# Attention over channels in float32r halves stacked four times along the contraction

## The chip, the cores and the metric

The kernel runs on one core of one Trainium2 chip. The metric is the device time of one execution in microseconds; the time of the kernel before is the median of three runs. Beside it there is one profiled execution with a trace of every instruction. The engines are named as in the profile: PE (TensorE, matrix products), PEld (its weight loads), DVE (VectorE), ACT (ScalarE), POOL (GpSimd) and SP (SyncE, which issues the transfers here).

## The reference

The program is a decoder of four layers with three sublayers each: an attention, a cross-attention and a feed-forward part. After each of them the rows are added to their input and normalized. `x` and the context `ctx` have the shape 64 x 64 x 256 (64 sequences of 64 rows). The change concerns the fifth sublayer, the cross-attention of the second layer, in which the 256 channels attend to each other and the 64 rows of a sequence are split into 8 heads of 8 rows:

```python
def _L1_xattn_ref(q, k, v, gamma):          # q = x, k = v = ctx_2048
    N_HEAD = 8
    B, Dq, Lq = q.shape                     # 64, 64, 256
    Dv, Lk = (v.shape[-2], v.shape[-1])
    h = N_HEAD
    dq = Dq // h                            # 8
    dv = Dv // h
    qh = q.reshape(B, h, dq, Lq)
    kh = k.reshape(B, h, dq, Lk)
    vh = v.reshape(B, h, dv, Lk)
    scale = 1.0 / jnp.sqrt(jnp.asarray(dq, dtype=q.dtype))
    qk = jnp.einsum('bhdq,bhdl->bhql', qh, kh) * scale
    sm = jax.nn.softmax(qk, axis=-1)
    ret = jnp.einsum('bhql,bhdl->bhdq', sm, vh)
    ret = ret.reshape(B, Dv, Lq)
    return gamma * ret
...
x = _layernorm(x + _L1_xattn_ref(x, ctx_2048, ctx_2048, L1_xattn_gamma), axis=-1)
```

There are 512 blocks (64 sequences x 8 heads). Each is a score matrix of 256 x 256 whose contraction is only 8 long.

## The kernel before

**Order of the whole.** The rows lie in eight groups of 512, each held in on-chip memory as `X[g]` (128 partitions, 4 tiles of 128 rows, 256 channels). The sublayers run one after the other: the first attention, then the first cross-attention and feed-forward together (`l0_both`), the second attention (`l1_attn`), then the attention over channels (`l1_xattn`) and its feed-forward (`l1_ffn`). Inside these functions the order of PE, ACT, DVE and (in `l0_both` and `l1_attn`) POOL is written out by hand: each engine works its instructions off in the order of the program, and one that waits holds up all behind it. The transfers on SP are placed by the scheduler, and SP too works them off in one queue.

**Tiles and blocks of the fifth sublayer.** A tile is 128 rows, or two sequences, or 16 blocks; there are 32. The 128 rows of PE's array are used as four strips of 32, one for each of four blocks at a time (index `r`), and the loop over `j` (0 to 3) goes through the rest. A step of the loop (L1652, `for step in range(n + 2)`) takes a new tile `step` and an old one `step - 2`; for each `j` there is one unit: two calls of `scored` (a half each, two strips for the new tile and the two others for the old one), then `weighted` for the unit before.

- `scored` (L1531) makes for the new tile the scores with the queries on the partitions (`sq`, L1547), two products of 128 x 256 a block, of which DVE takes the negated maximum of each row (`mc`, L1552). For the old tile it makes the transposed scores, keys on the partitions (`sk`, L1550), of which ACT takes the exponential (`e`, L1558).
- The maxima enter the transposed scores as a ninth row of the contraction: row 8 of each strip of the context's tile `cr` holds ones, row 8 of the rows' tile `xr` the negated maxima. `move` (L1561) brings them there: PE transposes `mc`, DVE copies it, SP stores it to memory and loads it back in its place. That happens one unit into the next step, so the old tile is two steps behind the new one.
- `weighted` (L1579) multiplies the exponentials with the values (`ret`, L1586; four blocks side by side, 32 columns of the array each), with a column of ones for the sums; ACT copies `ret` out at each `j` (L1590), and `store` writes the tile to memory.
- `load` (L1517) fetches a tile: 8 rows of context and of `x` a block, from `ctx` itself and from a copy of `X[g]` that is written to memory for it (`xd`, L1520). The four buffers of the tiles were cleared or set to one ahead (L1499, L1501).

All products here are float32. The trace records each of them as two, one for each half of the weights. All eight banks of the accumulators are one ring (`bank`, eight buffers): `sq`, `sk`, `ret` and the transposed maxima take the next free one.

**Around it.** In `l0_both` the feed-forward runs in units of 128 hidden columns, six a group (`HC`); `halved` (L1166) splits the turned rows into two float32r halves, `xhi` and `xlo`, in two buffers each. In `l1_attn` a loop of 12 iterations takes the eight groups through six stages. Each stage takes its memory from a pool, and the pool of `l1_both` waits, at its first write, for the last reader of what lay there before.

## Time and profile before

| | us |
|---|---|
| median of three runs | 4140.58 |
| lowest and highest run | 4131.2 and 4144.52 |
| the profiled execution | 4137.55 |
| its span from the first to the last instruction | 4135.8 |
| PE, PEld busy | 3900.5 (94%), 2594.9 (63%) |
| DVE, ACT, POOL busy | 2984.5 (72%), 2260.6 (55%), 1505.2 (36%) |

Busy time of the groups of the fifth sublayer, from the profile's costliest groups (a group's busy time counts overlapping instructions once):

| line | engine | what | count | busy us | mean ns |
|---|---|---|---|---|---|
| L1547 | PE | `sq` | 2048 records | 274.1 | 403 |
| L1550 | PE | `sk` | 2048 records | 253.4 | 394 |
| L1586 | PE | `ret` | 2048 records | 139.4 | 387 |
| L1552 | DVE | maxima | 512 | 317.5 | 683 |
| L1558 | ACT | exponentials | 512 | 265.6 | 609 |

PE's records overlap, as matrix products are pipelined and their ends are modelled: what one costs is seen in the distance between the starts of two, not in its duration. The same holds in part for DVE and ACT, where one instruction starts some 0.1 us before the modelled end of the last. A granted clock of 1.00 is the full one for PE, 0.50 is half. In the whole span it was 0.98 in the mean.

### The profile page before, as it was taken

How to read it: one execution, taken by the hardware profiler on the slowest of the kernel's cores; microseconds unless marked ns; L12 is line 12 of the kernel's file. 1: busy time of each engine (PE TensorE's matmuls, PEld its weight loads, DVE VectorE, ACT ScalarE, POOL GpSimd, SP SyncE). 2: the span in 40 equal slices, each digit the busy share in tenths (PEclk: the TensorE clock that was granted, in tenths of full speed). 3: DMA queues.
4: the chain of work that ended last, by engine and by line, in shares of the span. 5: the costliest groups of instructions: out<-in, count | busy, mean ns of one | idle time of the engine just before them, and what ended most of it. 6: DMA issues, size and time to landing. Idle time of an engine off the chain costs nothing.

```text
span 4135.8 us, 74789 instructions
## 1 busy us (share of the span) xinstructions
PE 3900.5 (94%) x28788; PEld 2594.9 (63%) x28808; DVE 2984.5 (72%) x5916; ACT 2260.6 (55%) x4654; POOL 1505.2 (36%) x1604
## 2 busy tenths in 40 slices
PE   8979988989998999989999999999999899999997
PEld 5646666666675555546666666666666666666765
DVE  6855658888684687877777777777776677777775
ACT  5645445667534577554444444444444476767765
POOL 4411121332441111115555555555543333433432
PEclk9989998999999999999999999999999999999999
DMA  2210012333200000031111111111121100000000
GB/s 73 85 35 16 16 55 56 75 79 72 78 1 13 1 1 1 11 133 29 29 27 26 27 31 27 27 26 27 31 72 54 47 22 22 24 24 22 23 20 11
DMA packets 112657, 149.68 MB, mean 36 GB/s; under 512 B 17636, under 2 KB 76196, under 8 KB 110888
## 3 DMA queue, kind: packets, MB, share of 16 engines
q1 hardware_dynamic: 111336, 143.27, 12.6%
q8 instruction: 230, 3.77, 0.4%
q10 hardware_dynamic: 960, 1.57, 0.2%
q14 instruction: 131, 1.07, 0.1%
HBM read 71.64 MB, written 30.95 MB: 25 GB/s over the span
## 4 chain that ended last, share of the span: by engine, by line
PE 43%; DVE 9%; ACT 2%; issue 1%; POOL 1%; DMA 0%; DVEq 0%; POOLq 0%; ACTq 0%
PE p L2116 19%; PE acc L2473 5%; PE acc L2739 4%; PE qT L561 2%; PE s L2411 2%; PE kT L561 1%; PE y L2441 1%; PE h L449 1%; PE yt L561 1%; PE s L2665 1%; DVE s L2672 1%; PE pt L561 1%; PE o L502 1%; PE y L2711 1%; DVE s L2671 1%
## 5 line engine op out<-in xcount | busy, mean ns | idle before, releaser
L1552 DVE TENSOR_REDUCE mc<-sq 128x2 f32<-128x512 f32 x512 | 317.5, 683 | 64.1 <-PE sk L1550 62.8
L555 POOL TENSOR_TENSOR rstd<-rstd,neg_half 128x1 f32<-128x1 f32 (+1 forms) x187 | 145.2, 777 | 600.1 <-DVE rstd L553 583.2
L1558 ACT ACTIVATE e<-sk 128x512 f32<-128x512 f32 x512 | 265.6, 609 | 113.1 <-PE sk L1550 91.8
L555 POOL TENSOR_TENSOR hrq<-hrq,neg_half 128x4 f32<-128x4 f32 (+1 forms) x192 | 234.4, 1221 | 246.4 <-DVE hrq L553 240.2
L1547 PE MATMUL sq<-l1x 32*128 32x256 f32 x2048 | 274.1, 403 | 4.9 <-DVE mc L1552 3.4
L555 POOL TENSOR_TENSOR hrk<-hrk,neg_half 128x4 f32<-128x4 f32 x160 | 187.8, 1174 | 228.4 <-DVE hrk L553 173.2
L1550 PE MATMUL sk<-l1x 32*128 32x256 f32 x2048 | 253.4, 394 | 0.5 <-DVE mc L1552 0.5
L2116 PE MATMUL p<-l3a_wq,xt 128*128 128x512 f32 x512 | 243.7, 599 | 9.7 <-DVE v L542 8.4
L2116 PE MATMUL p<-l3a_wk,xt 128*128 128x512 f32 x512 | 247.9, 607 | 0.0
L1547 PEld LDWEIGHTS sq<-l1x 32*128 32x128 f32 x2048 | 207.7, 193 | 57.7 <-DVE mc L1552 22.9
L2116 PE MATMUL p<-l3x_wq,xt 128*128 128x512 f32 x512 | 241.3, 594 | 0.8 <-DVE k L2577 0.8
L2739 PE MATMUL acc<-l3x_wo,yt 128*128 128x256 f32 x1024 | 235.7, 383 | 5.2 <-DVE yt L2723 3.5
L2116 PE MATMUL p<-l3a_wv,xt 128*128 128x512 f32 x512 | 233.2, 598 | 0.6 <-DVE k L542 0.4
L2473 PE MATMUL acc<-l3a_wproj,yt 128*128 128x256 f32 x1024 | 232.1, 380 | 0.6 <-DVE yt L542 0.3
L2473 PEld LDWEIGHTS acc<-l3a_wproj,yt 128*128 128x128 f32 x1024 | 194.1, 190 | 53.9 <-issue 29.2
L2739 PEld LDWEIGHTS acc<-l3x_wo,yt 128*128 128x128 f32 x1024 | 193.2, 191 | 44.2 <-issue 6.7
L1550 PEld LDWEIGHTS sk<-l1x 32*128 32x128 f32 x2048 | 189.4, 187 | 6.4 <-issue 2.9
L561 PEld LDWEIGHTS qT<-ident,q 128*128 128x128 f32 x1024 | 121.7, 141 | 98.4 <-issue 77.1
L2457 POOL TENSOR_TENSOR hry<-hry,neg_half 128x8 f32<-128x8 f32 x64 | 106.2, 1659 | 179.2 <-DVE hry L2453 174.7
L561 PE MATMUL qT<-ident,q 128*128 128x128 f32 x1024 | 156.7, 276 | 6.7 <-DVE hlo L413 5.4
L1586 PE MATMUL ret<-e,vt 128*32 128x256 f32 x2048 | 139.4, 387 | 18.9 <-DVE mc L1552 18.1
L2116 PEld LDWEIGHTS p<-l3a_wv,xt 128*128 128x128 f32 x512 | 92.1, 190 | 97.4 <-issue 82.0
(444 smaller groups left out, 10405.0 us busy)
## 6 DMA issues: line engine op xcount, KB each, us to landing
vs<-v SPq DMA_DIRECT2D x308, 128.0 KB
l3x_kv<-kv SPq DMA_DIRECT2D x28, 256.0 KB
x<-in_x SPq DMA_DIRECT2D x8, 512.0 KB
ct<-in_ctxT SPq DMA_DIRECT2D x8, 512.0 KB
cn<-in_ctx SPq DMA_DIRECT2D x8, 512.0 KB
l_x<-x SPq DMA_DIRECT2D x8, 512.0 KB
l1x<-in_ctx SPq DMA_DIRECT2D x128, 32.0 KB
l1x_x<-x SPq DMA_DIRECT2D x8, 512.0 KB
```

The source lines that it names most:

```text
L555: nc.gpsimd.tensor_tensor(out, out, self.neg_half[:, :n], ALU.pow)
L561: self.nc.tensor.transpose(ps[:, j * P : (j + 1) * P], blk, self.ident)
L1547: nc.tensor.matmul(ps[:, n, :], x_[rows, j, part], c_[rows, j, :], start=True, stop=True)
L1550: nc.tensor.matmul(ps[:, n, :], c_[rows, j, part], x_[rows, j, :], start=True, stop=True)
L1552: nc.vector.tensor_reduce(mc[new % 2][:, ra + k, 2 * j : 2 * j + 2], ps, AX.X, ALU.max, negate=True)
L1558: nc.scalar.activation(es[rb + k], ps, AF.Exp, scale=scale)
L1586: nc.tensor.matmul(ret[32 * r : 32 * r + 32, :], vt[i % 2][:, lc, 4 * r + j, :], es[r][:, lc, :], start=lc == 0, stop=lc == 1,)
L2116: self.nc.tensor.matmul(ps, lhs(c), w(c, cols), start=c == 0, stop=c == 1 and bias is None)
L2411: nc.tensor.matmul(ps[half(b), h * S : (h + 1) * S], qT[:, h % 4, half(b)], kT[:, h % 4, half(b)], start=True, stop=True,)
L2457: nc.gpsimd.tensor_tensor(r, r, self.neg_half[:, :8], ALU.pow)
L2473: nc.tensor.matmul(acc[:, :D], yts[h % 2][:, h // 2, :], wp[n // 8][:, (n % 8) * D : (n % 8 + 1) * D], start=n == 0, stop=n == 15,)
L2739: nc.tensor.matmul(acc[:, :D], yts[h % 2][:, h // 2, :], w.o[n // 8][:, (n % 8) * D : (n % 8 + 1) * D], start=n == 0, stop=n == 15,)
```

## The change

Rows and context of the fifth sublayer are no longer multiplied in float32. Each is split into two float32r halves, `hi` (the rounded value) and `lo` (what is left), and a block's contraction of 8 rows becomes 32: row `k` of four carries the half `k // 2` of `x` and the half `k % 2` of the context, so that one product of a strip sums all four combinations. The halves are made early and kept in memory: those of the context in the feed-forward stage of the first layer, those of `x` at the end of the second attention, by `halves_kept` (a cast on ACT, a subtraction on POOL, eight stores). `load` then needs eight transfers of 128 KB a tile. Nothing is cleared ahead any more, and a constant (`in8`) goes.

The maxima are no longer a row of the contraction. They are split into halves too (`mhi` by ACT, `mlo` by DVE, a store and a load each) and a product of its own lays them under both parts of `sk`: two rows of ones against the two halves, 512 columns.

The eight banks are divided: three for `sk` and the transposed maxima (tag `k`), two pairs for `sq` (tag `q`), one for `ret`. One reduction takes the maxima of a pair, that is of two blocks; `ret` of two units lies in one bank and is copied out every second time. The four blocks at a time are now neighbours, so `vt` and the stores change their indices.

```diff
+                if u == 1 or u >= 0 and u % HC == 3 and u // HC + 1 < self.n_groups:
+                    g = 0 if u == 1 else u // HC + 1
+                    self.halves_kept(self.ctx_halves[g], self.cns[g], wk, ("xhi", "xlo"), 2)
...
+    def halves_kept(self, dram, src, pool, tags, bufs):
+        nc = self.nc
+        hi, lo = (pool.tile([P, TG, D], F32R, tag=tag, name=tag, bufs=bufs) for tag in tags)
+        nc.scalar.copy(hi, src)
+        nc.gpsimd.tensor_tensor(lo, src, hi.bitcast(F32), ALU.subtract)
+        to = dram.rearrange("(t h q) (j c) -> h j q t c", t=TG, h=2, j=4)
+        for h, x in enumerate((hi, lo)):
+            for j in range(4):
+                self.load(to[h, j], x[32 * j : 32 * j + 32].bitcast(F32))
+
+    def halves_tiles(self, name):
+        return [self.tc.dram_tile([2 * NTOK // 4, 4 * D], F32, name=f"{name}{g}") for g in range(self.n_groups)]
...
+                if i >= 6:
+                    self.halves_kept(self.x_halves[i - 6], self.X[i - 6], wk, ("xh", "xl"), 2)
             for part in ends:
                 part()
+            for g in range(max(0, n - 2), n):
+                self.halves_kept(self.x_halves[g], self.X[g], wk, ("xh", "xl"), 2)
...
-        bank = lambda name: self.psum.tile([P, 2, D], F32, tag="b", name=name, bufs=8)
+        bank = lambda name, tag="k", bufs=3: self.psum.tile([P, 2, D], F32, tag=tag, name=name, bufs=bufs)
...
-        for t in cr:
-            nc.gpsimd.memset(t, 1.0)
-        for t in xr:
-            nc.vector.memset(t, 0.0)
+        mx = [wk.tile([P, 4, D], F32R, tag=f"mx{i}", name="mx", bufs=1) for i in range(2)]
+        ones = wk.tile([P, P], F32R, tag="ones", name="ones", bufs=1)
+        nc.scalar.activation(ones, self.ident, AF.Identity, bias=1.0, scale=0.0)
...
         def load(g, t):
-            i = (g * TG + t) % NB
-            if t == 0:
-                nc.sync.dma_start(out=xd[g].rearrange("(t p) d -> p t d", p=P), in_=self.X[g])
-            for r in range(4):
-                rows = slice(t * P + 32 * r, t * P + 32 * r + 32)
-                part = slice(32 * r, 32 * r + 8)
-                self.load(
-                    cr[i][part],
-                    ins["ctx"][g * NTOK + rows.start : g * NTOK + rows.stop, :].rearrange("(j d) c -> d j c", d=8),
-                )
-                self.load(xr[i][part], xd[g][rows, :].rearrange("(j d) c -> d j c", d=8))
-            self.load(xr[i][8:P:32].rearrange("r j q -> r (j q)"), none)
+            w = both[(g * TG + t) % NB].bitcast(F32)
+            for k in range(4):
+                for i, (src, h) in enumerate(((self.x_halves, k // 2), (self.ctx_halves, k % 2))):
+                    self.load(w[k:P:4, i, :], src[g][64 * t + 32 * h : 64 * t + 32 * h + 32, :])
...
+            if new is not None:
+                sq = self.psum.tile([P, 2, 2, D], F32, tag="q", name="sq", bufs=2)
...
+            for k, ps in enumerate(sks):
+                rows = group(rb + k, 2)
+                nc.tensor.matmul(
+                    ps, ones[rows], mx[old % 2][rows, j, :].unsqueeze(1).broadcast_to([2, 2, D]), start=True, stop=False
+                )
...
-                    nc.tensor.matmul(ps[:, n, :], c_[rows, j, part], x_[rows, j, :], start=True, stop=True)
-            for k, ps in enumerate(sqs):
+                    nc.tensor.matmul(ps[:, n, :], c_[rows, j, part], x_[rows, j, :], start=False, stop=n == 1)
+            if sq is not None:
                 nc.vector.tensor_reduce(
-                    mc[new % 2][:, ra + k, 2 * j : 2 * j + 2], ps, AX.X, ALU.max, negate=True
+                    mc[new % 2][:, ra : ra + 2, 2 * j : 2 * j + 2], sq, AX.X, ALU.max, negate=True
                 )
...
-            mt = wk.tile([P, P], F32, tag="mt", name="mt")
-            nc.vector.tensor_copy(mt, ps)
-            nc.sync.dma_start(out=md[i % NB], in_=mt)
-            self.load(
-                xr[i % NB][8:P:32].rearrange("r j q -> r (j q)"),
-                md[i % NB].rearrange("(r n) q -> r (n q)", r=4)[:, : 8 * P],
-            )
+            hi, lo = (wk.tile([P, P], F32R, tag=tag, name=tag, bufs=1) for tag in ("mhi", "mlo"))
+            nc.scalar.copy(hi, ps)
+            nc.vector.tensor_tensor(lo, ps, hi.bitcast(F32), ALU.subtract)
+            for h, mt in enumerate((hi, lo)):
+                nc.sync.dma_start(out=md[h][i % NB], in_=mt.bitcast(F32))
+                self.load(
+                    mx[i % 2][h:P:32].bitcast(F32).rearrange("r j q -> r (j q)"),
+                    md[h][i % NB].rearrange("(r n) q -> r (n q)", r=4)[:, : 8 * P],
+                )
...
-            ret = bank("ret")[:, 0, :]
+            if j % 2 == 0:
+                state["ret"] = bank("ret", "ret", 1)
+            ret = state["ret"][:, j % 2, :]
...
-            nc.scalar.copy(state[i][:, j, :], ret)
+            if j % 2 == 1:
+                nc.scalar.copy(state[i][:, j - 1 : j + 1, :], state.pop("ret"))
```

## The prediction

> **What bounds the kernel now.** I read the page's groups first, to find the sublayer that the diff rewrites; then its instructions by tile and in order of time, to get one steady unit; then short windows with the granted clock. The change touches the attention over channels (L1478 on). There PE, DVE and ACT each do 16 blocks a tile, and 32 tiles pass.
>
> ```profile
> L1552 DVE TENSOR_REDUCE mc<-sq x512: 671/681/693, 640.6 to 1070.1; 128x2 f32<-128x512 f32 x171
> L1558 ACT ACTIVATE e<-sk x512: 592/606/757, 660.0 to 1088.5; 128x512 f32<-128x512 f32 x171
> L1586 PE MATMUL ret<-e,vt x2048: 376/379/636, 666.4 to 1090.0; 128*32 128x256 f32 x187
> ...
> 756.59 0.35 SPq L1567 DMA_DIRECT2D l1x_m<-mt  x1
> 769.24 0.35 SPq L1567 DMA_DIRECT2D l1x_m<-mt  x1
> 781.88 0.34 SPq L1567 DMA_DIRECT2D l1x_m<-mt  x1
> ...
> 761.28 1.07 PE L1586 MATMUL ret<-e,vt 128*32 128x256 f32 x16
> 763.44 2.48 DVE L1552 TENSOR_REDUCE mc<-sq 128x2 f32<-128x512 f32 x4 [0.46 <-PE sk L1550]
> 763.59 2.06 ACT L1558 ACTIVATE e<-sk 128x512 f32<-128x512 f32 x4 [0.61 <-PE sk L1550]
> 764.36 1.07 PE L1586 MATMUL ret<-e,vt 128*32 128x256 f32 x16
> ```
>
> The stage runs from 640.6 to about 1090 us. A step without extras lasts 12.65 us (the maxima leave at 756.59, 769.24, 781.88), a unit (one j) 3.16. Within it four reductions take 2.48, four exponentials 2.06 plus a copy of 0.41, and `ret` 1.07. PE does the rest: its records stand 0.2155 us apart in rounds of four, 8 rounds (1.72 us) for the scores and 4 (0.86) for `ret`, with 0.11 at each turn between the two. So PE bounds the unit, DVE close behind. The whole of steps 2 to 31, from the first exponential at 660.0 to the last reduction at 1070.1, is 410 us or 3.42 a unit; 31 us of that are extras above 30 x 12.65.
>
> The windows then show what the clock does:
>
> ```profile
> core 0: us, PE busy (x) PEld busy (x) DVE busy (x) ACT busy (x) POOL busy (x), PEclk, DMA share, GB/s
> 644.10:647.50 3.40, 3.40 (x27) 3.40 (x25) 3.40 (x7) 0.00 (x0) 2.09 (x2) 0.50 0.00 0
> ...
> 650.90:654.30 3.40, 3.40 (x32) 3.23 (x34) 3.30 (x7) 0.00 (x0) 0.00 (x0) 0.50 0.09 23
> 654.30:657.70 3.40, 3.08 (x26) 1.99 (x20) 3.40 (x6) 0.00 (x0) 0.00 (x0) 0.99 0.03 6
> 657.70:661.10 3.40, 3.26 (x25) 3.12 (x27) 3.40 (x7) 1.08 (x2) 0.00 (x0) 0.51 0.00 0
> 661.10:664.50 3.40, 3.40 (x26) 2.19 (x23) 1.80 (x4) 1.19 (x2) 0.00 (x0) 0.50 0.07 19
> 664.50:667.90 3.40, 3.40 (x36) 1.65 (x28) 2.58 (x4) 2.17 (x4) 0.00 (x0) 0.50 0.01 5
> 667.90:671.30 3.40, 3.40 (x60) 2.16 (x55) 1.97 (x4) 2.26 (x5) 0.00 (x0) 0.99 0.02 5
> ```
>
> The last columns are clock, DMA share and GB/s. While only `sq` runs, PE is busy 3.08 of 3.40 us, yet the next stretch has half the clock; after x36 it is full again. Nearly every record here occupies a quarter of the array for 512 column steps (0.213 us, 0.427 at half clock). Summed by records over the trace's clock periods of 3.41 us (records at an edge in part), a period with at most 24 such records was followed by half clock, one with 25 or more by the full one; I found that in either state, with a few exceptions, most of them where 64-row products run. The old unit brings 48 records in 3.16 us, 52 a period.
>
> **The change, part by part.** Score products: 32 records a unit of 512 steps become 16 single passes of 256 steps, which is 8 record-equivalents. That one pass is enough I take from L1182, whose fp32r products of 512 columns stand 0.23 us apart. Weight loads don't hold it: four of 0.185 start together, and the next set 0.108 later (762.277 and 762.385). Added: four products a unit of 512 columns that lay the maxima under `sk`, two rows high (0.213 us, two at a time). `ret` stays: 16 records.
>
> Banks: `sk` has three, where all kinds shared eight. So the second `sk` bank of a half waits for the first exponential of the half before, and PE's queue behind it (`sq`, `sk`, then `ret`) waits too; ACT waits for that. I follow one unit at full clock from its first product at 0. Maxima to 0.213, first round of `sk` to 0.32; the last record of the first block starts there, and its exponential 0.436 later (0.543 in the trace from such a record to ACT, less one pass of 0.107): 0.76. It releases its bank after 0.597 and 0.056: 1.41. Maxima of the second half to 1.62, two rounds to 1.84, turn 0.11, `ret` 0.86, turn 0.11: **2.92 us**. DVE needs 2 reductions of 1024: L830 has this form at 1.20 alone, 1.12 in a row by the overlap of 0.08 that L1552 shows, so 2.24; ACT 2.06 and half a copy of 512 (L1391, 0.59), 2.36. Both fit.
>
> The same unit at half clock: maxima to 0.427, round to 0.64, exponential 0.53 later (0.74 in the half-clock stretch, less 0.213) at 1.17, released at 1.82, maxima to 2.25, rounds to 2.68, turn, `ret` 1.71, turn: **4.61 us**. The transposition of the maxima, once in four units, adds about 0.1 to either: 2.95 and 4.64.
>
> Now the records: 8 + 16 = 24 a unit, 28 if a two-row product counts as its whole strip of 32. At half clock the fullest 3.41 us hold `ret` (16) and 1.48 us of scores at half density, 7: 23, which is not 25. With the strips counted it is 26. Steps 0 and 1 bring `sq` alone, 4 equivalents in 2.24 us, so step 2 starts at half clock. No row shows a product of two rows, so both readings stay; I take two rows as two, since every other shape in the trace counts by its rows and columns. Then **the clock never comes back**, and the unit is 4.64.
>
> Sum for that: steps 2 to 31, 120 x 4.64 = 557 against 410: +147; DVE's extras now hide in its 2.4 us of idle time a unit (31 more if they didn't). Steps 32 and 33, 8 x 4.61 = 37 against 20: +17. Steps 0 and 1 go by DVE, 16 x 1.12 against 19.5: -1.6.
>
> The join before the stage:
>
> ```profile
> 638.03 2.07 ACT L804 ACTIVATE x<-z,nmr,rstd 128x256 f32<-128x256 f32 x4 [1.63 <-DVE nmr L802]
> 640.13 0.23 DVE L185 CAST ident<-ident 128x128 bf16<-128x128 f32 x1 [2.14 <-ACT x L804]
> ```
>
> DVE's first write into the next stage's memory waits for the last reader of the attention's pool. That will be the stores of the last two groups' halves: two casts of 1.05 (L991), two subtractions of 2.36 on POOL (L1403), four issues of 0.35, 1.6 to land. 640.1 becomes about 649: **+9** (6 to 11). Before it, four clearings of 0.91 on DVE (L1501) go, three of them inside the chain that ends the first feed-forward stage's last group: -3 (0 to -4). The other halves, 8 in the feed-forward stage and 6 in the attention, cost ACT 1.05, POOL 2.36 and SP some 8 issues each; they fall in units without exponentials, where ACT shows gaps of 1 to 4 us, and in ACT gaps of 1.5 to 1.9 before L1413: +2, and +15 if that cover were gone. On SP their stores wait for ACT and POOL; behind them stand copies and weight loads that waited up to 41 us there already. Loads of a tile grow from 256 KB to 1 MB but in 8 issues of 0.3 us instead of 9, a step ahead. The maxima now take two pairs of DMAs; a store is followed by its load after 1.55 us (769.24 to 770.79), so they land 7.5 to 9.2 us into a step of at least 11.8: nothing.
>
> -1.6 + 147 + 17 + 9 - 3 + 2 = **+170**: 4137.55 + 170 = 4308 for a profiled execution, whose own time before was 4137.55; the median of the runs stands 3 above it, so **4310**, by itself 4270 to 4345.
>
> [...]
>
> **The rivals.** *The clock swings* (two-row products count as strips, 26 records in the best period): it comes back within some units and falls at each extra. Half the units each way, (3.20 + 4.64)/2 = 3.92 with extras: 470 against 410, tail +10, join and rest +7: 4218 by the runs' median. For it: 26 is above the bound, barely. Against: the placing of 3.41 us must be almost exact.
>
> *The clock stays full*, the faster side: 120 x (2.95 - 3.16) = -25, extras absorbed -5, tail +3, first steps -2, join and rest +8: -21, so 4120 (4095 to 4130). It decides as soon as periods hold 25 records at half clock early and no unit is longer than about 3.4 us. For it: 24 to 28 records in 2.95 us are 28 to 32 a period on average. Against: the old extras made units of 3.5 to 6 us in every group of four steps.
>
> *One pass is not one pass*: if 32-row fp32r products of 256 columns still took four, the unit is 0.213 + 0.65 + 0.543 + 0.653 + 0.213 + 0.86 + 0.11 + 0.86 + 0.11 = 4.21 at full clock (48 records, so it stays): +95, +14, +8: 4258. L1182 speaks against it.
>
> **How the numbers follow.** Half clock throughout 0.47, swinging 0.25, full clock 0.23, four passes 0.05. The range takes the first, second and fourth cases and most of the third: 4105 to 4345. Faster by over 0.3% (12 us, about what this kernel's runs tell from no change) is the full clock's share, 0.22; within 0.3%, the edges of the second and third, 0.05; slower 0.73.
>
> **What would show it.** A granted clock of 0.5 in windows from about 650 to the stage's end, units of 4.6 us, ACT and DVE idle behind PE `sk`. PE records of single passes 0.11 us apart at full clock, 0.21 at half. DVE's first reduction at 647 to 651. Wrong if the clock column reads 1.00 in steps 3 to 31, whatever the time then is.

## The result and the profile after

The changed kernel takes **4280.91 us** (median of 4 runs, 4276.26 to 4296.9) against 4137.24 before (4 runs): 1.0355 times as long, 95% interval 1.0338 to 1.0372. The profiled execution has a span of 4274.5 us, 138.7 more than before, at a mean granted clock of 0.939 instead of 0.980. The forecast was 4310, slower, so side and size are right; but several of its terms were wrong, in opposite directions, so that the size is in part luck.

The instructions of the channel attention by tile (shortest/median/longest duration, first and last start):

```profile
L1562 DVE TENSOR_REDUCE mc<-sq x256: 1202/1225/1227, 667.5 to 1183.5; 128x4 f32<-128x1024 f32 x128
...
L1600 PE MATMUL ret<-e,vt x2048: 379/634/636, 693.2 to 1226.4; 128*32 128x256 f32 x187
L1568 ACT ACTIVATE e<-sk x512: 591/596/599, 687.5 to 1223.8; 128x512 f32<-128x512 f32 x171
```

The stage began at 640.6 and now begins at 667.5; its last `ret` stood at 1090.0 and now stands at 1226.4. So the stage begins 27 us later and lasts 110 longer; behind it 2 more are lost. The median `ret` record has grown from 379 to 634 ns on the same operands: the clock. The windows, in the columns of the prediction's, show it:

```profile
core 0: us, PE busy (x) PEld busy (x) DVE busy (x) ACT busy (x) POOL busy (x), PEclk, DMA share, GB/s
...
650.00:700.00 50.00, 24.45 (x158) 14.77 (x158) 27.85 (x28) 11.20 (x21) 11.43 (x13) 0.50 0.68 203
700.00:750.00 50.00, 43.20 (x367) 24.12 (x363) 25.37 (x23) 25.11 (x48) 1.37 (x5) 0.50 0.27 73
...
950.00:1000.00 50.00, 43.03 (x386) 24.77 (x382) 33.87 (x51) 26.01 (x50) 20.35 (x22) 0.56 0.37 98
1000.00:1050.00 50.00, 39.98 (x571) 23.01 (x560) 42.81 (x47) 39.15 (x76) 11.90 (x13) 1.00 0.50 141
...
1100.00:1150.00 50.00, 40.05 (x572) 23.22 (x568) 42.62 (x47) 38.94 (x75) 11.82 (x15) 1.00 0.50 138
...
1200.00:1250.00 50.00, 42.64 (x258) 25.42 (x253) 18.35 (x41) 20.81 (x35) 13.33 (x14) 0.73 0.41 123
```

The clock is 0.50 from 639.5 to 994.5 us without a break, 1.00 from there to 1178.8, and 0.50 again in the two steps without `sq`: 375 us of this stage at half clock, where the kernel before had 31. A step (four units) lasts 20.1 us in the first part and 12.6 to 13.0 in the second: at full clock it is hardly shorter than the 12.65 of before, although the scores' rounds on PE have shrunk from 1.72 us a unit to some 0.85 (two of maxima at 0.21, four at 0.11). What holds it is seen in one unit at half clock, in order of time (start, length, in brackets the idle time before and what ended it):

```profile
802.35 0.79 PE L1550 MATMUL sk<-mx,ones 2*128 2x512 f32 x1 [0.68 <-ACT e L1568]
802.36 0.58 PE L1557 MATMUL sq<-l1x 32*128 32x256 f32 x2
...
803.50 1.94 PE L1600 MATMUL ret<-e,vt 128*32 128x256 f32 x16
805.37 0.79 PE L1550 MATMUL sk<-mx,ones 2*128 2x512 f32 x2
```

PE stands 0.68 us once a unit: the second half's second `sk` finds no bank until an exponential is through. The waits of PE from 700 to 950 us (half clock) and from 1000 to 1170 (full) say it in sums, with the same 0.7 in both:

```profile
PE sk L1550 <- ACT e L1568: 34.0, 50, 0.7
...
PE sk L1550 <- ACT e L1568: 30.6, 50, 0.7
PE sk L1550 <- DVE mlo L1577: 2.5, 3, 0.8
```

At the join, in order of time:

```profile
660.19 1.98 SPq L669 DMA_DIRECT2D l1x_x<-xl  x4
662.22 3.03 SPq L669 DMA_DIRECT2D l1x<-l1x_x  x5
...
664.70 1.00 DVE L185 CAST ident<-ident 128x128 bf16<-128x128 f32 x1 [13.89 <-DMA l1x<-l1x_x]
...
666.70 0.81 PE L1557 MATMUL sq<-l1x 32*128 32x256 f32 x8 [23.80 <-DMA l1x<-l1x_x]
```

The cast that waited 2.14 us before waits 13.89 now. Its line names a load, but ACT's and POOL's first writes into the new stage's memory start with it (664.60, 664.67), just after the last packets of the stores of the halves (1 KB each; the loads' have 4 KB) have ended at about 664. So I read the wait as one for those stores. The first product waits until 666.70, for the first tile's loads, which SP issues directly behind the last of the stores.

### The profile page after: what moved, and what is told of

Its sections match the earlier page's. It is cut to its first block, busy times and chain, and to the rows that moved or that the text cites. A ratio compares the mean times of both kernels' runs of the same rounds, so it can differ in the third digit from the quotient of the medians.

```text
span 4274.5 us, 71519 instructions
## 1 busy us (share of the span) xinstructions
PE 3946.4 (92%) x27252; PEld 2573.5 (60%) x27272; DVE 2993.8 (70%) x5656; ACT 2294.9 (54%) x4639; POOL 1539.6 (36%) x1607
## 4 chain that ended last, share of the span: by engine, by line
PE 41%; DVE 8%; ACT 2%; issue 1%; POOL 1%; DMA 0%; DVEq 0%; POOLq 0%; ACTq 0%
PE p L2131 19%; PE acc L2488 5%; PE acc L2754 4%; PE qT L561 2%; PE s L2426 2%; PE kT L561 1%; PE y L2456 1%; PE yt L561 1%; PE h L449 1%; PE s L2680 1%; DVE s L2687 1%; PE pt L561 1%; PE o L502 1%; PE y L2726 1%; DVE s L2686 1%
## 5 line engine op out<-in xcount | busy, mean ns | idle before, releaser
L1562 DVE TENSOR_REDUCE mc<-sq 128x4 f32<-128x1024 f32 x256 | 310.1, 1222 | 154.8 <-PE sq L1557 107.0
L1568 ACT ACTIVATE e<-sk 128x512 f32<-128x512 f32 x512 | 277.9, 594 | 187.3 <-PE sk L1560 185.6
L1550 PE MATMUL sk<-mx,ones 2*128 2x512 f32 x512 | 212.9, 627 | 85.0 <-ACT e L1568 80.7
L1550 PEld LDWEIGHTS sk<-mx,ones 2*128 2x128 f32 x512 | 91.7, 242 | 200.6 <-ACT e L1568 182.6
L1600 PE MATMUL ret<-e,vt 128*32 128x256 f32 x2048 | 198.1, 523 | 0.0
L1557 PE MATMUL sq<-l1x 32*128 32x256 f32 x1024 | 168.5, 418 | 29.9 <-DMA l1x<-l1x_x 23.8
L1560 PE MATMUL sk<-l1x 32*128 32x256 f32 x1024 | 194.0, 369 | 0.0
L2472 POOL TENSOR_TENSOR hry<-hry,neg_half 128x8 f32<-128x8 f32 x64 | 106.3, 1661 | 179.0 <-DVE hry L2468 171.2
L1560 PEld LDWEIGHTS sk<-l1x 32*128 32x128 f32 x1024 | 152.8, 260 | 9.8
```

The source lines that it names most:

```text
L1550: nc.tensor.matmul(ps, ones[rows], mx[old % 2][rows, j, :].unsqueeze(1).broadcast_to([2, 2, D]), start=True, stop=False)
L1557: nc.tensor.matmul(sq[:, k, n, :], x_[rows, j, part], c_[rows, j, :], start=True, stop=True)
L1560: nc.tensor.matmul(ps[:, n, :], c_[rows, j, part], x_[rows, j, :], start=False, stop=n == 1)
L1562: nc.vector.tensor_reduce(mc[new % 2][:, ra : ra + 2, 2 * j : 2 * j + 2], sq, AX.X, ALU.max, negate=True)
L1568: nc.scalar.activation(es[rb + k], ps, AF.Exp, scale=scale)
L1600: nc.tensor.matmul(ret[32 * r : 32 * r + 32, :], vt[i % 2][:, lc, 4 * j + r, :], es[r][:, lc, :], start=lc == 0, stop=lc == 1,)
```

## The experiments

Twelve kernels ran. "Share" below is my own sum: rows x columns x column steps of all products in a clock period of 3.41 us, over what 128 x 128 cells (the largest product of the traces) could do in that time at the clock granted. A column step is taken from the distances between records: at full clock float32 records of 256 columns, which count as 512 steps, stand 0.216 us apart, and bfloat16 ones of the same width 0.109. The period is read from the clock in the profiles' records: it changes at whole multiples of 3.413 us (639.5 to 994.5 are 104 of them, 994.5 to 1178.8 are 54, and in the kernel before 654.3 to 657.8 is one). An "extra" is work inside a step that is not the step's own: normalizing a group, or preparing the next stage.

### Two states, and who changes them

After this result the question was why the clock came back at 994.5. The periods around that moment in the changed kernel:

```profile
984.20:987.60 3.40, 3.17 (x28) 1.52 (x27) 3.23 (x10) 1.28 (x3) 0.00 (x0) 0.50 0.41 117
987.60:991.10 3.50, 2.87 (x20) 2.29 (x21) 3.47 (x5) 2.33 (x6) 3.16 (x3) 0.50 0.64 191
991.10:994.50 3.40, 3.40 (x28) 1.91 (x26) 0.44 (x2) 1.40 (x2) 3.32 (x4) 0.50 0.14 39
994.50:997.90 3.40, 2.73 (x49) 1.76 (x47) 2.45 (x2) 2.76 (x5) 0.30 (x1) 1.00 0.13 23
```

In the third row (990.66 to 994.5, share 0.91) stand eight full-array transpositions of the feed-forward's preparation (`rows`, 2.02 us) and a whole `ret`. The next row has the full clock, and keeps it. The first test brings such work on purpose.

```diff
+ if step == 2:
+     busy = bank("ret", "ret", 1)
+     for _ in range(6):
+         nc.tensor.matmul(busy, self.ident, self.X[0][:, 0:2, :], start=True, stop=True)
```

> Six dead fp32 products of 128x512 over the whole array (of the identity and rows that lie there, into the bank of ret, read by nobody) stand at the start of step 2; nothing else differs from the changed kernel. Theory now: the clock has two steady states in this stage, and the one in which step 2 begins lasts. The six take about 10 us at half clock, which fills the array for several clock periods; then the clock is 1.00 from step 2 to the last steps, 30 steps of the 12.8 us that the changed kernel shows after 994.5 us instead of 497 us in all: 4281 - 114 + 8, 4165 to 4185. Rival, the prediction's swinging clock: units that grow to 5 us with an extra drop the clock, which then stays at 0.50 for most of the stage: 4240 or more.

It took 4278.6 in the profiled run (4339.2 in the other, which has no trace): no gain. The clock did rise, and fell again:

```profile
682.90:686.30 3.40, 3.40 (x8) 1.62 (x9) 1.97 (x2) 0.00 (x0) 0.00 (x0) 0.50 0.32 96
686.30:689.70 3.40, 3.40 (x10) 1.43 (x8) 0.00 (x0) 0.00 (x0) 0.00 (x0) 1.00 0.73 206
689.70:693.10 3.40, 2.36 (x24) 1.33 (x22) 2.07 (x2) 1.90 (x4) 0.00 (x0) 1.00 0.05 18
693.10:696.60 3.50, 3.03 (x24) 1.97 (x28) 2.27 (x4) 1.86 (x5) 0.00 (x0) 0.51 0.17 44
```

The third row is the first unit of step 2, which has no `ret` yet: share 0.26, and half clock follows. The place was badly chosen. So the same six products once more, behind the first `ret` of step 3:

> The changed kernel with its two-row maxima products, and the six dead products of 128x512, now after the first ret of step 3 (in the first try they stood before any ret; the clock came up and fell after 6.8 us, while the units had no ret). Theory of two steady states: the clock is 1.00 from about 710 us until an extra makes one period too thin (the 32-row run fell at 842), and then 0.50 until the feed-forward's turn; 9 to 11 steps at 12.7 instead of 20.1: 4195 to 4225. If the state lasts through the extras: 4165 to 4185. Rival: two-row units can't hold the full clock before the extras are over, it falls within 20 us: 4280 to 4295.

```profile
700.00:750.00 50.00, 41.63 (x458) 22.54 (x450) 29.83 (x28) 29.51 (x58) 1.78 (x6) 0.85 0.30 80
...
800.00:850.00 50.00, 39.10 (x548) 22.49 (x545) 43.89 (x49) 37.82 (x73) 13.76 (x16) 0.99 0.53 141
850.00:900.00 50.00, 43.19 (x367) 23.86 (x367) 35.39 (x43) 24.94 (x48) 22.65 (x22) 0.50 0.36 93
...
950.00:1000.00 50.00, 39.98 (x570) 23.21 (x567) 42.83 (x47) 38.83 (x75) 12.88 (x15) 1.00 0.53 143
...
1050.00:1100.00 50.00, 43.19 (x366) 23.86 (x362) 26.98 (x24) 24.95 (x47) 1.19 (x4) 0.50 0.34 89
```

Full clock for 133 us (715 to 848), with nothing but the six products added; half after a thin period (share 0.29); full at 930, when the feed-forward's turn came; half from 1012 to the end, again after a thin period (0.32). The profiled run took 4270.3, the other 4211.0: the full state was lost to single thin periods, and the untraced run, with a mean clock of 0.962 instead of 0.940, must have kept it longer. **Both states hold themselves in this kernel**: its own units neither raise the clock (share at most 0.69 while it stayed half) nor lose it (at least 0.37 while it stayed full).

### Rows or strips

The products that lay the maxima become 32 rows high; `mx` is cleared once before.

```diff
- rows = group(rb + k, 2)
+ rows = group(rb + k)
- ... mx[old % 2][rows, j, :].unsqueeze(1).broadcast_to([2, 2, D])
+ ... mx[old % 2][rows, j, :].unsqueeze(1).broadcast_to([32, 2, D])
```

> The products that lay the maxima under sk are 32 rows high instead of two; 30 of them are zero, so the sums are the same. If the clock counts rows, a unit brings 28 quarter-array records instead of 24, and the fullest 3.41 us of a unit at half clock hold 26 or 27 instead of 23: the clock comes back to 1.00 within some steps of 687 us, and the time is 4165 to 4210. If it counts strips of 32 (then the changed kernel had the 26 already and stayed at half clock), or if 26 isn't enough, the clock is 0.50 until about 994 us as before and the time 4281 within 0.3%.

4174.88 us (1.0089 of before, 1.0059 to 1.0118) and 106 less than the changed kernel, for 30 rows of zeros. The clock rises at 723 with nothing but the units' own work, falls at 845.9, 883.5 and 910.8 after periods that an extra thinned (shares 0.31, 0.36 and 0.16), and rises again, at 856 and 904 on the units' own work:

```profile
719.60:723.00 3.40, 3.40 (x34) 1.82 (x32) 1.31 (x2) 1.78 (x4) 0.00 (x0) 0.50 0.00 0
723.00:726.40 3.40, 2.72 (x45) 1.58 (x39) 2.47 (x3) 2.20 (x5) 0.00 (x0) 1.00 0.09 28
...
842.50:845.90 3.40, 1.87 (x21) 0.74 (x19) 3.26 (x10) 1.83 (x4) 2.21 (x3) 1.00 0.72 207
845.90:849.30 3.40, 2.77 (x26) 2.02 (x30) 3.40 (x6) 1.72 (x4) 3.40 (x3) 0.50 0.28 72
```

So two rows counted as two. The next kernel asks the same from the other side: plain fp32 makes each score and maxima product four passes (in the kernel before a score product is two records, 0.2155 us apart, where the changed kernel has one of 0.11), and PE is busy for 47.4 of the 50 us from 1000 to 1050.

```diff
- both = [self.weight(f"l1x{i}", F32R).rearrange("p (i n) -> p i n", i=2) for i in range(NB)]
+ both = [self.weight(f"l1x{i}").rearrange("p (i n) -> p i n", i=2) for i in range(NB)]
- mx = [wk.tile([P, 4, D], F32R, tag=f"mx{i}", name="mx", bufs=1) for i in range(2)]
+ mx = [wk.tile([P, 4, D], F32, tag=f"mx{i}", name="mx", bufs=1) for i in range(2)]
- ones = wk.tile([P, P], F32R, tag="ones", name="ones", bufs=1)
+ ones = wk.tile([P, P], F32, tag="ones", name="ones", bufs=1)
```

> The halves, the maxima and the ones are held as plain fp32, so that each score product and each maxima product takes four passes; values, loads, banks and order are the same. Theory (work on the array in each 3.41 us decides the clock): 48 or more records in a unit keep the clock at 1.00 from step 3 on, and the unit is the 4.2 us of the prediction's four-pass case, or 4.5 if the maxima too take four passes one after the other; 120 units of it are 504 to 540 against 497: 4270 to 4330, with clock 1.00 although the array works four times as long on the scores. If the clock were lost by the wait for banks, it stays at 0.50 and the unit is 7 us or more: 4500 or more.

5008.06 us, a miss: I had not thought that four passes of two-row products take PE's time (a unit is 10.1 us at half clock, 5.6 to 5.7 at full) and, counted by rows, bring hardly any work. Two neighbouring periods and the one that lost the clock:

```profile
1003.60:1007.00 3.40, 3.40 (x25) 1.39 (x27) 1.22 (x1) 1.70 (x3) 0.00 (x0) 0.50 0.00 0
1007.00:1010.40 3.40, 3.31 (x22) 1.75 (x14) 1.03 (x1) 0.31 (x2) 0.00 (x0) 0.50 0.03 5
...
1353.80:1357.20 3.40, 2.82 (x29) 1.64 (x23) 1.66 (x2) 1.42 (x3) 0.00 (x0) 1.00 0.72 210
```

PE is busy for 3.40 of 3.40 us in the first, and the clock is half, as it was for 600 us on end (1357 to 1958). Counted by strips of 32 its fullest periods reach a share of 0.91 and still stay half, where others rise at 0.73; counted by rows they reach 0.71. That settles the rows. No run changes the columns alone, but without them the sum no longer sorts the periods: if every product counts with all 128 columns, periods at half clock with sums up to 2.23 stay half, and others rise at 0.83 and 0.95 (in the first try at the order, below, and in the second with added products).

Over the profiles of the changed kernel and the runs up to here, by rows and columns: at half clock, periods up to 0.73 were followed by half, the lowest that raised the clock inside the stage had 0.73; at full clock, periods up to 0.36 lost it, from 0.37 on they kept it. 0.73 at half clock is 0.365 at full: the same work in 3.41 us, 23.4 of the prediction's records. The later runs, of other orders and banks, blur both edges by 0.02, and a few single periods there rose at 0.66 to 0.72.

### The banks

First the cheap cure, another order: `ret` between the two halves of a unit, so that it runs in the wait for the bank.

```diff
- es = {**scored(new, old, j, 0), **scored(new, old, j, 1)}
+ es = scored(new, old, j, 0)
+ if before is not None:
+     weighted(*before)
+ es.update(scored(new, old, j, 1))
```

> The eight products of ret (of the unit before) are issued between the two halves of a unit's scores instead of after them, so that they run while the second half's bank waits for its exponential. Theory: the half-clock unit is 4.92 because PE stands 0.68 us in that wait and ret follows it; with ret in the wait it is 0.43 + 0.43 + 0.11 + 1.71 + 0.11 + 0.43 + 0.43 + 0.11 = 3.76 at half clock and some 2.5 at full clock, where ACT with 2.36 and DVE with 2.24 bound it. The clock still comes back only with the feed-forward's turn of the first group, half way: 15 steps of 15.4 and 15 of 10.6, and a shorter tail: 4150 to 4190. Rival: ACT's exponentials wait for banks just as long in the new order (the wait only moves), unit 4.7 to 4.9 at half clock and 4270 to 4290.

4427.62 us, a miss. Most of it is the clock: it rises at 1022.8, when the feed-forward's turn comes, but falls at 1036.5 after a period with a share of 0.36, and is 0.50 in all the rest of the stage, where the changed kernel has 1.00 for half of its steps. The steps themselves are 20.4 and 23.2 us instead of 20.1. PE's waits from 700 to 1000 us:

```profile
PE sk L1550 <- ACT e L1568: 30.0, 48, 0.7
PE sk L1550 <- DMA mx<-l1x_m: 25.2, 7, 4.1
```

The first line is the old wait, only moved: the second half of a unit is now followed at once by the first half of the next, which waits. The second is new: `weighted` ends with a tile's five stores, and these now stand ahead of the maxima's stores on SP (805.02 to 807.13, then the maxima at 807.57). The second try lags `ret` by one unit more, on the 32-row kernel:

```diff
- if before is not None:
-     weighted(*before)
+ if before[0] is not None:
+     weighted(*before[0])
...
- before = (old, j, es) if old is not None else None
+ before = [before[1], (old, j, es) if old is not None else None]
```

> Base is the kernel with 32-row maxima products (4175). ret is issued between the halves of a unit, but it is that of the unit before the last, so that it waits for no exponential that is still to come (in the run that put the last unit's there, ret waited for the second half's exponentials). Banks and two-bank maxima stay. Theory: the bank wait is covered by ret, unit 0.21 + 0.36 + 0.11 + 0.86 + 0.11 + 0.21 + 0.36 + 0.11 = 2.33 for PE, ACT 2.36 to 2.5 bounds it; step 10.0 to 10.8, thirty steps 310 to 340 instead of 412, time 4075 to 4110. Rival: another wait takes its place, step 12 or more, time above 4155.

No gain: 4174.5 in the profiled run, 4212.6 in the other (4178.7 and 4171.0 for the two of its base). The step at full clock is 13.1 instead of 12.6, and `sk` waits for `e` 67.8 us between 700 and 1050, 100 times (59.7 and 98 in the base): the wait only moves again, which I should have read from the first try. Then the banks themselves, on the 32-row kernel:

```diff
- bank = lambda name, tag="k", bufs=3: self.psum.tile([P, 2, D], F32, tag=tag, name=name, bufs=bufs)
+ bank = lambda name: self.psum.tile([P, 2, D], F32, tag="b", name=name, bufs=8)
- sq = self.psum.tile([P, 2, 2, D], F32, tag="q", name="sq", bufs=2)
+ sq = [bank("sq"), bank("sq")]
...
- if j % 2 == 0:
-     state["ret"] = bank("ret", "ret", 1)
- ret = state["ret"][:, j % 2, :]
+ ret = bank("ret")[:, 0, :]
```

> Base is the kernel with 32-row maxima products (4175). One part of the change is undone: all banks come from one ring of eight again, the maxima are taken bank by bank (four reductions a unit) and ret is copied each unit. Theory: at full clock the changed kernel's unit of 3.08 is set by the bank of the second half, which waits for an exponential (0.68 us a unit), not by any engine; with eight banks PE has some 1.9 us of work, ACT 2.06 + 0.41 and DVE 4 x 0.62, so the unit is 2.6 to 2.8, a step 10.6 to 11.2 instead of 12.6, the thirty steps 330 to 355 instead of 412, and the time 4090 to 4125. Rival: the path from scores to exponential to ret sets the unit whatever the banks; the step stays 12.4 to 12.7 and the time 4165 to 4185.

4130.43 us (0.9987 of before, 0.9975 to 0.9998). From 910 to 1050 us, where the clock of both is mostly full, the base and this kernel wait so:

```profile
PE sk L1552 <- ACT e L1570: 25.0, 41, 0.7
PE sk L1552 <- DVE mlo L1579: 1.6, 2, 0.8
```

```profile
PE ret L1600 <- DVE mc L1564: 4.4, 18, 0.4
PE sk L1552 <- DMA mx<-l1x_m: 4.2, 3, 2.5
...
PE sk L1552 <- ACT e L1570: 1.4, 2, 0.7
```

25.0 us of waiting for banks become 1.4, a step without extras 10.0 to 10.6 instead of 12.6, and the stage from first exponential to last `ret` 389.5 us instead of 438.8 (before: 430.0). The theory's mechanism holds; its step of 10.6 to 11.2 is met only in steps without extras. With them steps are 12 to 16 us: DVE is busy for 334 of 375 us, and an extra also thins PE's periods, so that the clock falls 11 times between 700 and 1050, each time for one or two periods. How much of those steps is DVE and how much the clock was not separated. Whether the banks alone would have done is asked by the same edit on the changed kernel, with its two rows:

> The changed kernel with only the banks undone (one ring of eight, four single-bank reductions, ret copied each unit); the maxima products are two rows high as in the changed kernel. It tells whether the banks alone decided the clock. Theory (periods of 3.41 us at half clock need about 0.73 of the array, counted by rows): a unit of PE alone at half clock is 0.43 + 0.43 + 0.43 + 0.43 + 1.71 and some 0.4 of turns, 3.84; 24 records are 0.67 on average and 23 or 0.72 in the fullest period, just short, so the clock stays 0.50 until the feed-forward's turn and then is 1.00: 15 steps of 15.4 instead of the 11.5 of the run with 32 rows: 4175 to 4205. Rival: the wait for banks alone kept the clock down, and without it two rows are enough: 4130 to 4145.

4166.36 us (1.0074, 1.0054 to 1.0094), between the two. At half clock its fullest periods have 0.72 to 0.75, exactly the edge: some rise and some stay. The clock changes about as often as with 32 rows, some twenty times in the stage, but each fall lasts longer:

```profile
700.00:1050.00 350.00, 311.32 (x3758) 180.75 (x3750) 295.44 (x523) 253.04 (x544) 96.41 (x108) 0.74 0.48 131
```

```profile
700.00:1050.00 350.00, 298.25 (x4133) 177.71 (x4133) 322.00 (x575) 275.49 (x600) 104.13 (x119) 0.92 0.52 141
```

The first is this kernel (clock 0.74), the second the ring with 32 rows (0.92). So each part alone gives back about as much (115 us for the banks, 106 for the rows), and both 151. A ring of four pairs, with one reduction and one exponential of 1024 columns, goes too far the other way:

```diff
- bank = lambda name, tag="k", bufs=3: self.psum.tile([P, 2, D], F32, tag=tag, name=name, bufs=bufs)
+ pair = lambda name: self.psum.tile([P, 2, 2, D], F32, tag="b", name=name, bufs=4)
...
+ e = wk.tile([P, 2, 2, D], F32, tag="e", name="e", bufs=5)
+ nc.scalar.activation(e, sk, AF.Exp, scale=scale)
```

> As the ring of eight with the moved halves, but the eight banks are a ring of four pairs: the two blocks of a half lie in one pair, so that one reduction and one exponential each take 1024 columns. DVE's maxima cost 2.24 to 2.4 a unit instead of 2.48, ACT's exponentials some 1.9 instead of 2.06. Theory: DVE with its extras sets the unit when no bank does, so 120 units gain 0.1 to 0.24: 4075 to 4100. Rival: one exponential over two blocks starts only when both are there and frees both late, so that PE waits for pairs as it waited for banks in the changed kernel; unit 2.9 or more, 4130 or more.

4157.35 us (1.0057, 1.004 to 1.0074) against 4129.26 for the same kernel with single banks. PE's waits from 750 to 1050 us:

```profile
PE ret L1612 <- ACT e L1581: 41.5, 58, 0.9
PE mt L1588 <- DVE mc L1575: 28.9, 21, 4.0
```

The rival was right that one exponential over two blocks comes late, but it is `ret` that waits for it, not the banks (`sk` waits 7.5 us for `e`).

### Before the stage

In the first feed-forward stage POOL's group of `rstd` shows what the halves cost there (idle time and what ended it at the end of the line; before, all 106.3 us of it were waits for DVE's `rstd`):

```profile
L555 POOL TENSOR_TENSOR rstd<-rstd,neg_half 128x4 f32<-128x4 f32 x14 | 14.2, 1014 | 84.9 <-DVE rstd L553 76.7 <-DMA l1x_c<-xhi 8.2
```

Both are moved, on the 32-row kernel: `half_kept` does what `halves_kept` does for two of the four tiles of a group, in tiles of its own; the attention keeps the first five groups, and the last three come in the next stage's loop, in the memory of `l1_xt`, which is free there (so `first.load` goes to step 3).

```diff
- self.halves_kept(self.ctx_halves[g], self.cns[g], wk, ("xhi", "xlo"), 2)
+ self.half_kept(self.ctx_halves[g], self.cns[g], wk, 2 * a)
...
- if i >= 6:
+ if 6 <= i < n + 3:
...
+ if step < 3:
+     g = self.n_groups - 3 + step
+     self.halves_kept(self.x_halves[g], self.X[g], None, (0, 1), 1)
```

> Base is the kernel with 32-row maxima products (4175). Two stores are moved, in different stages. (1) The halves of the attention's last three groups are made and stored in the first three steps of the next stage, behind the first loads of rows, in memory that outlives the attention; so nothing in the attention's own memory is read by a store at the join. Theory: the join of 25.2 us is the landing of 4 stores of 512 KB, and falls to 8 to 12, 14 to 17 us less. (2) The halves of the context in the feed-forward stage have tiles of their own, two of its tiles at a time, instead of the two buffers of xhi and xlo. Theory: ACT, DVE and POOL wait there for stores of halves (POOL 8.2 us in rstd alone), and the stage's last gate product comes at 531 to 536 instead of 542.5. Both: 4145 to 4160. Rival for (2): the casts and subtractions themselves in the queues of ACT and POOL cost it, and the last gate stays at 540 to 544; then 4157 to 4165.

The profiled run took 4163.7, the other 4204.8; the boundaries tell more than these. The last gate product of the first feed-forward stage comes at 533.1 (544.4 in its base, 530.3 before), inside the expected 531 to 536. But 4.4 of these 11 us are not the edit's: this trace's first gate product stands at 247.5, the base's at 251.9, and so far the two kernels hold the same instructions. From first to last gate product the stage takes 285.6 us, against 292.5 in the base and 278.7 before. So about half of the cost is back; the rival, the casts and subtractions themselves, may be the rest, which no run separates. The first reduction comes at 649.7 instead of 669.1: 4.4 from the earlier start, 7 from this stage and 8 from the join, half of what I expected. DVE's cast waits 2.1 us as before the change, but the attention itself is still 12.6 us longer than before from its first `kv` to the stage's first reduction. At its end DVE's `nmr` waits 6.7 us for POOL's `rstd`, which has the earlier groups' subtractions in its queue, and the first product still waits for the loads of its tile:

```profile
PE sq L1572 <- DMA l1x<-l1x_x: 15.6, 1, 15.6
```

SP issues these loads from 643.98, directly behind the stores of the earlier groups (the last at 643.39). Moving these groups out as well, with the ring of eight:

```diff
- if 6 <= i < n + 3:
+ if 6 <= i < 8:
...
- if step < 3:
-     g = self.n_groups - 3 + step
+ if step < self.n_groups - 2:
+     g = 2 + step
```

> The 32-row maxima and the ring of eight (4130), with the halves of the context in tiles of their own in the first feed-forward stage (11 us in the run before), and the rows' halves of groups 2 to 7 made in the first six steps of the next stage instead of in the attention, where POOL's subtractions stood before its rstd and stores before the join. Theory: 4130 - 11 - 8 to 18, as the join goes back from 25 to some 5 to 8: 4100 to 4112, faster than the kernel before. Rival: the casts, subtractions and 48 more stores in the first steps cost there what they save: 4115 to 4125.

4129.26 us, a miss: nothing beyond the ring of eight. The first reduction comes at 643.0 instead of 668.3 (4 of these 25 us are an earlier start again), and the first steps give all of it back: PE waits there (655 to 750 us) for

```profile
PE sk L1565 <- DMA mx<-l1x_m: 21.8, 6, 8.3
```

the maxima, whose stores and loads share SP's queue with 48 more stores. With the three groups of the run before instead of six, and all else as here:

> The 32-row maxima and the ring of eight (4130), with the context's halves in tiles of their own in the first feed-forward stage and only the attention's last three groups of rows made in the next stage's first three steps, in which two run without exponentials. Theory: in the run with 48 stores there the maxima's loads stood behind them on SP (PE waited 21.8 us for them); with 24, two thirds of them before the first maxima are needed, the 10 us of the feed-forward stage and 5 to 9 us of the join remain: 4110 to 4122. Rival: the steps give the join back again, and only the feed-forward stage counts or not even that: 4120 to 4132.

**4124.79 us, 0.9974 of before (0.9963 to 0.9985)**: 11 us under the kernel before and 156 under the changed one. That is what the rival expected (4120 to 4132), not the theory (4110 to 4122), and its interval overlaps that of the ring of eight alone (0.9975 to 0.9998). The rows' halves give back part of what they save here too: the first reduction comes 15 us earlier than with the ring alone, the last `ret` 4, and PE still waits 12.6 us for the maxima between 650 and 750 us.

## Why the prediction was right, and where not

Term by term, as boundaries of the two profiled executions give it:

| term | predicted | measured |
|---|---|---|
| steps 2 to 31 | +147 | +86 (687.5 to 1183.5 = 496, against 410) |
| steps 32 and 33 | +17 | +23 (43 against 20) |
| steps 0 and 1 | -1.6 | +0.6 |
| everything up to the first reduction | +8 (9, 2 and -3) | +27 |
| behind the stage | 0 | +2 |
| sum | +170 | +139 |

- **The clock falls and stays half**: right to 994.5 us, and for the reason given. Two rows count as two (with 32 the clock rose at 723), the fullest period has 0.69 or 22 records, where I had 23, and the edge lies at 23.4, not at 25.
- **"The clock never comes back"** is the step that failed. The sum counted as work only what the units bring. The feed-forward's turn, which PE does inside this stage, made one period full enough, and from there the units held the full clock: 14.7 steps at 12.76 instead of 18.56 are the 85 us that are missing. By the sign that the prediction gave for being wrong, a clock of 1.00 in steps 3 to 31, half of them speak against it. That two-row units would hold the full clock was in the price of neither this case nor the swinging one, which had it fall at each extra; the case of a full clock was counted unlikely for the same extras. But at full clock no unit of the changed kernel is longer than 3.44 us, extras included, and no period there falls below 0.37. Where an extra did thin one (in the second run with added products and in the 32-row run), the clock fell.
- **The unit** was taken too short. At half clock 4.61 was worked out and 4.92 measured, with the transposition 5.02 on average instead of 4.64: over 15.3 steps some 24 us more. From the first maxima to the bank's release 1.91 instead of 1.82, from there to `ret` 1.15 instead of 0.97, `ret` and turn 1.87 instead of 1.82. The second is the largest: after the waiting bank's maxima three rounds of products stand (802.74, 802.94, 803.16) where I had two, since the late bank's two come behind its neighbour's. At full clock the same three are 1.41, 0.67 and 1.00: 3.08 where I had 2.92.
- **The bank wait** was right: it is in every unit, 0.68 us, and with a ring of eight, where it is gone, a step without extras falls to 10 us. That the change moves PE's work out of the way and puts this wait in its place is why even the full-clock steps gain nothing.
- **One pass is one pass**: products stand 0.11 us apart at full clock (1053.35, 1053.45, 1053.57), 0.21 at half.
- **The join**, +9, was 17.6 (from 7.6 to 25.2 us between the attention's last `o` and the first reduction), and the first reduction stands at 667.5 where the prediction looked for it at 647 to 651. I had counted four issues and one landing, not the 36 stores of 128 KB that SP issues from 639.3 to 661.6, nor the first tile's loads behind them. In every kernel here that stores halves up to the join, the first reduction comes 5.2 to 5.9 us after the first of these loads is issued (6.5 with four passes).
- **The other halves**, +2, cost 12 us at the first feed-forward stage's last gate product (530.3 to 542.7), and more than that in the stage itself: this trace's first gate product stands 4 us earlier than before, so the stage is 16.5 us longer (13 to 14 in the other traces with these halves). That is the case that the prediction priced at +15, with ACT's and POOL's work not covered. The trace shows one wait of 8.2 us for a store of halves; the 32-row kernel shows none on POOL's `rstd` and is nearly as slow (13.8 us longer than before), so the cause stays open beyond the 7 us that tiles of their own give back. Six came back in a shorter passage to the attention (23.3 to 17.2 us, of which I had 3), and the attention itself is 3 longer.

The 32 us between the forecast for a profiled execution, 4308, and the measured 4276 are thus -61 in the long steps, +19 before the stage and some +10 in the rest. That they partly cancel is luck.

That PE had work did not hold the clock by itself: with fp32 products PE was busy 3.40 of 3.40 us at clock 0.50, and 30 rows of zeros in one kind of product raised the clock although PE's waits for banks stayed at up to 0.7 us. Nor did short waits move it: the same 0.7 us wait stood in every unit of both states of the changed kernel, and its clock changed only at thin or full periods (shares 0.91 at 991.1, 0.26 at 1175.4).

## What to carry to other kernels

Before TensorE's work is made cheaper, add up what is left in each 3.41 us (the clock period of these traces), by rows and columns of the array: here a stage that fell below the edge (a share of 0.73 at half clock, 0.37 at full) ran its products at half clock for 375 us (a step of 20.1 us instead of 12.8), and the "saved" passes were what had held the clock (0.99 in the mean from 700 to 1050 us before the change). Count the banks as well as an engine's time: with three banks for a product that an exponential must release, the unit here was the chain through that engine and back (0.68 us of waiting in each, and 3.08 us at full clock against 3.16 before, though the scores' rounds took half as long). And work moved to another stage brings its stores along (at the join DVE's cast waited 13.89 us instead of 2.14); look at what stands behind them on SP and in the buffers they hold. When boundaries of two traces are compared, check first whether they start alike: here the same instructions came 4 us earlier in some traces than in others.

## What the runs showed of the hardware

In these profiles the granted clock has two states that both held on their own in the same loop (0.50 for 355 us, then 1.00 for 184). At full clock, periods of 3.41 us with a share of up to 0.36 lost it, and from 0.37 on they kept it; at half clock, periods of up to 0.73 stayed half, and the lowest that raised the clock had 0.73 (in the later runs both edges are blurred by 0.02, and a few single periods rose at 0.66 to 0.72). Rows in use counted, also with zeros in them: 30 rows of zeros took the time from 4281 to 4175 us, while four passes over two rows kept PE busy 3.40 of 3.40 us at clock 0.50. Columns were changed alone in no run; the sum sorts the periods only with them in it. Which state the loop kept hung on single periods: one full one (0.91) gave the changed kernel 184 us of full clock, one thin one (0.36) took it from the first try at the order after 14.
